# Second chunk's first unit of queries and keys by seven block products, its token sums made earlier

## The chip, the cores and the metric

The kernel runs as one program on one core of a Trainium2 chip. The metric is the device time of one execution in microseconds (us), the median of several runs. The engines are named as the profile names them: PE (matrix multiplication; PEld is its weight load), DVE (vector), ACT (scalar, activation functions), POOL and SP. SP only starts DMA transfers here. "SPq" is its queue of transfers.

## The reference, cut to what matters

The input is two sequences of 1024 tokens with 512 features, in float32. One block is computed:

```
xn = layernorm(x)
q, k, v = xn @ Wq.T + bq, xn @ Wk.T + bk, xn @ Wv.T + bv       # 32 heads of 16
s = softmax(causal(q k^T / 4)) v, heads joined, @ Wo.T + bo
g = silu(xn @ W_base.T + b_base + lora)                        # top 2 of 8 rank-16 experts
out = x + s * g
```

All large products are float32 products of a 512 x 512 weight with the tokens.

## The kernel before

**Chunks, units and steps.** Each sequence `b` is cut into two chunks `c` of 512 tokens, and the heads into four groups `oc` of eight. A unit `(b, oc, c)` is the attention of one head group over one chunk of queries. Its work is cut into steps: a unit with c = 0 has 5 steps, a unit with c = 1 has 13. The order of the first units is (0,0,0), (0,1,0), (0,0,1), (0,1,1): they take steps 0 to 4, 5 to 9, 10 to 22 and 23 to 35. In every step `n` the main loop issues, in this order, the score products (`scores(n)`, line 1392) with their two exponentials on ACT (line 1401), the products with the values of the step before (`values(n - 1)`, line 1442), the causal masks of step n on DVE (`masked(n)`, two multiplications `pt<-pt,causal`, only in steps on the diagonal), and then `fill(n)`. Every engine works through its own instructions in the order in which they were issued.

**Fill.** `fill(n)` (line 1298) puts tasks into the step: tasks with a cost in PE time, chosen by due step, and then tasks without one, which are DVE work and transfers. Projections (queries, keys, values, gate and output) are such tasks. They use a pool of two PSUM tiles (`mm_tile`, tag "mm"), so that a product can begin only when the tile of the product before the last has been read.

**Two ways to project queries and keys.** `qk_task` (line 377) makes the queries `pq` with four groups of four matmuls of 512 columns, the keys `pk` likewise, and ACT writes `qT` (two activations) and `kT` (one) from PSUM. `qk_blocks_task` (line 665) gets the same 2 x 2 block result with seven block products of 256 columns in place of eight, from sums of weight blocks (`four_sums`, four DVE operations on the tile `wqk`, by `qk_weights_task`, which also stores them with a transfer `kept<-wqk`) and sums of token blocks (`sums_task`, four DVE operations `asum2`, `asum1`, `asum0`, `asum3` of 128 x 512). DVE puts the products together:

```
p1 = product("q1", at(0, 0))
ve.tensor_scalar(keys[0], p1, bias, None, ALU.add)
add(q[0], product("q2", at(0, 1)), keys[0], less)
s = yield from sums_of(k)
add(keys[0], product("q6", s[1]), keys[0])
add(q[1], product("q7", s[2]), keys[0])
p5 = product("q5", s[0])
add(keys[0], p5, keys[0])
add(keys[1], p5, q[1])
add(keys[0], product("q3", s[3]), keys[0])
add(q[1], product("q4", at(1, 1)), q[1], less)
later.append((now[0] + 1, apart))
```

`apart` (line 705) is two activations on ACT, one after the other in place, that part `qT` into the two halves that the scores read. It is issued one step later, after that step's exponentials.

**Who uses which.** Before the change the first three units are projected whole: (0,0,0) by `first_task`, (0,1,0) and (0,0,1), which are `units[1:3]`, by `qk_task`. All others go through `stage` and `qk_blocks_task`. Block stages stand in `groups` (line 454); stages of one group share one set of token sums, made by the group's first stage. The first group is the values of chunk (0,1), a block product too (`p1` to `p7`), and the unit (0,1,1).

**The tokens of chunk (0,1).** `layernorm_task` normalizes them, turns them on DVE, writes them to a scratch tensor and reads them back in two halves as `xnT` (line 294, four transfers `xnT<-scr` for each half). `asum2` needs the first half alone, `asum1` the second half too.

Of the kernel before, what the change touches and what calls it, by code (L numbers as in the profile page):

```python
# [25 lines left out]
KC = D // P  # L26
# [54 lines left out]
def direct(ctx, tc, sound, x, wq, wk, wv, wo, wb, wa, wg, wB, bq, bk, bv, bo, bb, out):  # L81
# [34 lines left out]
    def load_qk(oc):  # L116


        t = sb.tile([P, 4 * KC, P], F32, tag="wqk", bufs=2, name=f"wqk{oc}")
        for n, src in enumerate((wq, wk)):  # L120
            nc.sync.dma_start(
                out=t[:, n * KC : n * KC + KC],
                in_=src.rearrange("(kc p) o -> p kc o", p=P)[:, :, oc * P : oc * P + P],
            )
        return t
# [79 lines left out]
    MM = 0.853  # L205
# [5 lines left out]
    turned_at, now = {}, [0]  # L211
# [165 lines left out]
    def qk_task(b, oc, c):  # L377

        xnT = xnTs[b, c]
        qk_begun.append((b, oc, c))  # L380
        pq = mm_tile("pq")
        for k in range(KC):
            matmul(
                pq, lhsT=wqks[oc][:, k, :], rhs=xnT[:, k, :], start=k == 0, stop=k == KC - 1
            )
            if k < KC - 1:
                yield MM
        qT = sb.tile([P, 2, C], F32, tag="qT", bufs=3, name=f"qT_{b}_{oc}_{c}")
        for par in range(2):
            nc.scalar.activation(  # L390
                qT[:, par], pq, AF.Identity, bias=bq_half[:, par, oc : oc + 1],
                scale=half[:, par : par + 1],
            )
        qTs[b, oc, c] = qT
        yield MM
        pk = mm_tile("pk")
        for k in range(KC):
            matmul(
                pk, lhsT=wqks[oc][:, KC + k, :], rhs=xnT[:, k, :], start=k == 0, stop=k == KC - 1
            )  # L400
            if k < KC - 1:
                yield MM
        kT = sb.tile([P, C], F32, tag="kT", bufs=4, name=f"kT_{b}_{oc}_{c}")
        nc.scalar.activation(kT, pk, AF.Identity, bias=bk_sb[:, oc : oc + 1])
        kTs[b, oc, c] = kT
        qk_done[b, oc, c] = now[0]
        yield MM
# [25 lines left out]
    def v_task(b, i):  # L433
# [18 lines left out]
    weights = {"v": (wv, bv_sb), "gate": (wb, bb_sb), "out": (wo, bo_sb)}  # L452

    groups = (
        [("v", 0, 1), ("qk", 0, 1, 1)],
        [("gate", 0, 0), ("qk", 0, 0, 2), ("qk", 0, 0, 3)],
        [("qk", 0, 1, 2), ("gate", 0, 1), ("qk", 0, 1, 3)],
        [("v", 1, 0), ("qk", 1, 0, 0), ("qk", 1, 0, 1)],
# [12 lines left out]
    combined, kept_at, b_diff, sums, sums_at, issued_at, ended = {}, {}, {}, {}, {}, {}, [0]  # L471
# [3 lines left out]
    def four_sums(at, to):  # L475

        ve.tensor_tensor(to[1], at[0, 1], at[0, 0], ALU.subtract)
        yield PAUSE
        ve.tensor_tensor(to[3], at[1, 1], at[0, 1], ALU.subtract)
        yield PAUSE  # L480
        ve.tensor_tensor(to[2], at[1, 1], to[1], ALU.subtract)
        yield PAUSE
        ve.tensor_tensor(to[4], at[1, 0], to[2], ALU.subtract)
# [41 lines left out]
    def qk_weights_task(n):  # L525

        oc = n % KC
        if n >= 2:
            wqks.append(load_qk(oc))
        w = wqks[n]  # L530
        sums = w[:, 2 * KC :]
        if n >= KC:
            nc.sync.dma_start(out=sums, in_=qk_kept[oc])
        else:
            for _ in range(3 if n >= 2 else 0):
                yield WAIT
            yield from four_sums(
                {(i, j): w[:, 4 * j + 2 * i : 4 * j + 2 * i + 2] for i in range(2) for j in range(2)},
                {t: sums[:, 2 * t - 2 : 2 * t] for t in range(1, 5)},
            )  # L540
            qk_kept[oc] = dram.tile([P, 2 * KC, P], F32, tag=f"kept_qk{oc}", bufs=1, name="kept")
            nc.sync.dma_start(out=qk_kept[oc], in_=sums)
        qk_ready[n] = now[0] + (2 if n >= KC else 0)
        yield WAIT
# [6 lines left out]
    def sums_task(k):  # L551

        at = tokens(k)
        s = [None] * 4

        def ahead(n):
            while k and made[k - 1] < n:
                yield WAIT

        def place(n):  # L560
            s[n] = sb.tile([P, 2, BK], F32, tag=f"sum{n}", bufs=1, name=f"asum{n}")
            return s[n]

        yield from ahead(4)
        ve.tensor_tensor(place(2), at(0, 0), at(1, 0), ALU.subtract)
        yield PAUSE
        ve.tensor_tensor(place(1), at(1, 1), s[2], ALU.subtract)
        yield PAUSE
        yield from ahead(5)
        ve.tensor_tensor(place(0), s[1], at(0, 0), ALU.add)  # L570
        yield PAUSE
        yield from ahead(6)
        ve.tensor_tensor(place(3), at(0, 1), s[1], ALU.subtract)
        group = group_of[stages[k]]
        sums[group], sums_at[group] = s, now[0]
# [291 lines left out]
    qk_begun = [(0, 0, 0)]  # L867
# [217 lines left out]
    units = [(b, oc, c) for b in range(NB) for oc in range(KC) for c in range(NC)]  # L1085
# [5 lines left out]
    plan, starts = [], {}  # L1091
# [50 lines left out]
    def normalized(b, c):  # L1142
        return sum(n < now[0] for n in posts.get((b, c), []))

    def stage(task, what, due, cost, takes, uses, ready, frees=()):

        k = stages.index(what)
        if what == groups[group_of[what]][0]:
            summed[k] = Task(
                due, sums_task(k), 0.0,  # L1150
                ready=lambda: ended[0] >= k - 1 and ready(),
            )

        def prepared():
            if what[0] == "qk":
                return now[0] > qk_ready.get(what[1] * KC + what[3], now[0])
            return issued_at.get((k, 1), now[0]) < now[0]

        staged[k] = Task(
            due, task(k), cost, takes=takes, uses=uses, frees=frees,  # L1160
            ready=lambda: ended[0] == k and ready() and prepared(),
        )
# [3 lines left out]
    for b in range(NB):  # L1166
        for c in range(NC):
            s0 = starts[b, 0, c]
            xn = [("xnT", b, c)]
# [3 lines left out]
            else:  # L1173
                Task(
                    s0 - 12 if b else -9, layernorm_task(b, c), 0.0, after=s0 - (40 if c == 0 else 30) if b else -9,
                    takes={"x": 1, "xnT": 1}, frees={"x": 1},
                )
            turned_ = lambda u=(b, c): now[0] > turned_at.get(u, now[0]) + 3
            for oc in range(KC):
                takes = {"qT": 1, "kT": 1}  # L1180
                if (b, oc, c) in units[1:3]:
                    Task(
                        starts[b, oc, c] - 1, qk_task(b, oc, c), 8 * MM, takes=takes, uses=xn,
                        ready=lambda u=units[units.index((b, oc, c)) - 1], t=turned_: u in qk_begun
                        and t(),
                    )
                elif oc or b or c:
                    stage(
                        qk_blocks_task, ("qk", b, c, oc), starts[b, oc, c] - 2, 7 * MM, takes, xn,
                        turned_,  # L1190
                    )
            if not b and not c:
                room["v"] -= 1
                for t in range(TT):
                    Task(
                        s0 + (1, 3, 5, 3)[t], v_task(b, t), 4 * MM, uses=xn + [("xnT", "wv")],
                        ready=turned_,
                    )
                Task(
                    3, combine_task("v", wv_sb), 0.0, after=5, uses=[("xnT", "wv")],  # L1200
                )
                for n, name in enumerate(("gate", "out")):
                    Task(
                        (20, 31)[n], combine_task(name), 0.0, after=(9, 22)[n], takes={"xnT": 1},
                        frees={"xnT": 1}, ready=lambda n=n: len(combined) > n,
                    )
                for n in range(2 * KC):
                    Task(
                        (20, 13, 26, 32)[n] if n < KC else -9, qk_weights_task(n), 0.0, after=9,
                        ready=lambda n=n: n < 2 or (  # L1210
                            now[0] > qk_done.get(((n - 2) // KC, (n - 2) % KC, 1), now[0])
                            and len(qk_ready) >= n
                        ),
                    )
            else:
                stage(values_task, ("v", b, c), s0 + (5 if c else 1), 14 * MM, {"v": 1}, xn, turned_)
# [4 lines left out]
                ready=turned_,  # L1221
# [3 lines left out]
                ready=lambda u=(b, c): now[0] > projected_at.get(u, now[0]),  # L1225
# [11 lines left out]
            else:  # L1237
                before = starts[b, KC - 1, c] + 2
                Task(len(plan) - 9, bases_task(b, c), 0.0, after=before - 12, takes={"xnT": 2})
                n = len(units) - 3  # L1240
# [3 lines left out]
                    ready=lambda: sum(len(x) for x in posts.values()) == len(units) - 1,  # L1244
                )
                for t in range(TT - 1):
# [9 lines left out]
                    ready=lambda b=b, c=c: normalized(b, c) == KC - 1,  # L1256
# [3 lines left out]
                    ready=lambda: posted.count(TT - 1) == 2,  # L1260
# [702 lines left out]
```

## Time and profile before

| what | us |
|---|---|
| median of 3 runs (601.55, 601.68, 602.28) | 601.68 |
| the profiled execution | 601.97 |
| its span, first to last instruction | 600.2 |
| PE busy in the span | 588.7 |
| DVE busy | 391.6 |
| ACT busy | 319.2 |

The time of an execution is 1.8 us more than the span of its instructions. Rows of a timeline give start, duration, engine, line, operation and tiles; "x8" rows are several instructions taken together, and square brackets hold the idle time of the engine before and what ended it. A float32 matmul has two records. The unit (0,0,1) is projected in the fill of step 8, from 59.07 to 66.05 us; the scores of step 8 start at 56.94, those of step 9 at 66.05, and those of step 10, the first that read the new queries, at 69.86.

### The profile page before, as it was taken

What the parts mean: (1) busy time and instruction counts of PE and PEld (TensorE: products, weight loads), DVE (VectorE), ACT (ScalarE), POOL (GpSimd) and SP (SyncE); (2) the same over time, 40 slices, a digit from 0 to 9 for tenths busy, and PEclk for the clock granted to TensorE, in tenths of its full rate; (3) what the DMA queues carried; (4) which work ended last, traced back from release to release, by engine and by line L of the source; (5) the groups of instructions that cost most, each with busy time, mean ns of one, the idle gap of its engine ahead of it and who ended that gap; (6) DMA issues with size and microseconds to landing.
All of it is one profiled execution on the core that took longest, in us unless ns stands there. A gap on an engine that the chain in (4) does not pass through costs nothing.

```text
span 600.2 us, 18801 instructions
## 1 busy us (share of the span) xinstructions
PE 588.7 (98%) x8327; PEld 281.9 (47%) x8327; DVE 391.6 (65%) x821; ACT 319.2 (53%) x368; POOL 9.2 (2%) x26
## 2 busy tenths in 40 slices
PE   8999999999999999999999999999999999999994
PEld 7335344544445544444346544453444454455551
DVE  4546788287488857566487866664547865785742
ACT  2445454656666565556655545455565565565631
POOL 2000000000001000000000000000000000000000
PEclk9999999999999999999999999999999999999998
DMA  8523474247101534234133062430121013401101
GB/s 266 140 69 122 136 261 149 55 142 211 39 4 48 189 109 129 89 101 135 36 111 90 22 194 80 159 125 6 37 71 52 11 51 98 161 21 55 58 20 58
DMA packets 57929, 58.66 MB, mean 98 GB/s; under 512 B 8312, under 2 KB 49280, under 8 KB 57456
## 3 DMA queue, kind: packets, MB, share of 16 engines
q1 hardware_dynamic: 57824, 57.38, 31.0%
q8 instruction: 67, 1.10, 0.8%
q14 instruction: 22, 0.18, 0.1%
q10 hardware_dynamic: 16, 0.00, 0.0%
HBM read 43.24 MB, written 14.12 MB: 96 GB/s over the span
## 4 chain that ended last, share of the span: by engine, by line
PE 93%; DMA 3%; DVE 3%; issue 0%; SPq 0%; ACT 0%; DVEq 0%
PE s L1392 25%; PE av L1442 23%; PE p L220 20%; PE q L220 13%; PE ph L220 3%; PE po L220 2%; PE pv L220 2%; DMA kept<-wqk 1%; PE pq L220 1%; PE pk L220 1%; DMA dens<-den 1%; DMA x<-in_x_dram 1%; DVE wqk L55 1%; PE pq_first L330 1%; PE h L220 1%; PE pk_first L330 0%
## 5 line engine op out<-in xcount | busy, mean ns | idle before, releaser
L1401 ACT ACTIVATE pt<-s 128x1024 f32<-128x1024 f32 x288 | 279.2, 1021 | 230.2 <-PE s L1392 228.6
L1392 PE MATMUL s<-qT,kT 32*128 32x512 f32 (+3 forms) x1680 | 166.5, 490 | 0.1
L1442 PE MATMUL av<-pt,v 128*32 128x512 f32 (+3 forms) x1680 | 154.3, 467 | 0.9 <-DVE pt L55 0.6
L55 DVE TENSOR_TENSOR pt<-pt,causal 128x512 f32<-128x512 f32 (+1 forms) x160 | 90.6, 582 | 64.9 <-ACT pt L1401 64.7
L1392 PEld LDWEIGHTS s<-qT,kT 32*128 32x128 f32 x1680 | 72.4, 184 | 68.3 <-issue 47.3
L1442 PEld LDWEIGHTS av<-pt,v 128*32 128x32 f32 x1680 | 39.7, 108 | 93.6 <-issue 61.4
L220 PE MATMUL p<-wt,asum 128*32 128x256 f32 x960 | 58.2, 379 | 0.0
L220 PE MATMUL q<-asum,wqk 128*32 128x256 f32 x832 | 50.8, 379 | 0.0
L220 PEld LDWEIGHTS p<-wt,asum 128*32 128x32 f32 x960 | 31.0, 110 | 26.5 <-issue 9.9
L220 PE MATMUL q<-xnT,wqk 128*32 128x256 f32 x624 | 40.2, 379 | 0.0
L220 PEld LDWEIGHTS q<-asum,wqk 128*32 128x32 f32 x832 | 27.0, 110 | 25.1 <-issue 8.4
L55 DVE TENSOR_TENSOR g<-p,g 128x512 f32<-128x512 f32 x28 | 18.9, 686 | 16.8 <-PE p L220 16.5
L220 PEld LDWEIGHTS q<-xnT,wqk 128*32 128x32 f32 x624 | 20.9, 110 | 18.9 <-issue 5.1
L220 PE MATMUL p<-w,xnT 128*32 128x256 f32 x448 | 27.3, 379 | 0.0
L55 DVE SCALAR_TENSOR_TENSOR kT<-q,kT 128x256 f32<-128x256 f32 x39 | 16.5, 422 | 14.9 <-PE q L220 14.3
L55 DVE TENSOR_TENSOR x<-p,x 128x512 f32<-128x512 f32 x21 | 14.2, 688 | 15.0 <-PE p L220 15.0
L55 DVE TENSOR_TENSOR v<-p,v 128x512 f32<-128x512 f32 x21 | 14.1, 687 | 11.2 <-PE p L220 11.2
L220 PE MATMUL p<-w,asum 128*32 128x256 f32 x320 | 20.0, 379 | 0.0
L220 PEld LDWEIGHTS p<-w,xnT 128*32 128x32 f32 x448 | 14.5, 110 | 11.1 <-issue 3.3
L747 ACT ACTIVATE sg<-g 128x512 f32<-128x512 f32 x16 | 10.0, 630 | 16.9 <-DVE g L55 16.9
L707 ACT ACTIVATE qT<-qT,half 128x512 f32<-128x512 f32 x26 | 18.8, 722 | 0.4
L220 PE MATMUL ph<-wag_sb,xnT 128*32 128x136 f32 x512 | 17.2, 279 | 0.0
(132 smaller groups left out, 479.4 us busy)
## 6 DMA issues: line engine op xcount, KB each, us to landing
wt<-kept SPq DMA_DIRECT2D x40, 256.0 KB
x<-in_x_dram SPq DMA_DIRECT2D x16, 256.0 KB
scr<-sq SPq DMA_DIRECT2D x6, 512.0 KB
xnT<-scr SPq DMA_DIRECT2D x24, 128.0 KB
w<-in_wb_dram SPq DMA_DIRECT2D x12, 256.0 KB
xr<-in_x_dram SPq DMA_DIRECT2D x12, 256.0 KB
out_dram<-x SPq DMA_DIRECT2D x12, 256.0 KB
w<-in_wv_dram SPq DMA_DIRECT2D x9, 256.0 KB
```

The source lines that it names most:

```text
L55: return getattr(self.engine, name)(*args, **named)
L220: nc.tensor.matmul(o[j : j + 32], lhsT=lhsT[:, j : j + 32] if len(lhsT.shape) == 2 else lhsT[:, j // 32], rhs=rhs, start=start, stop=stop,)
L330: nc.tensor.matmul(ps[:, cols], lhsT=w[:, k, :], rhs=xnT[:, k, cols], start=k == 0, stop=k == KC - 1)
L707: nc.scalar.activation(qT[:, par], qT[:, 0], AF.Copy, scale=half[:, par : par + 1])
L747: nc.scalar.activation(sg, g(i, j), AF.Tanh, scale=0.5)
L1392: nc.tensor.matmul(ss[s // 2][:, s % 2, col : col + w], lhsT=kT[rows, kt % TT * P : kt % TT * P + P], rhs=qTs[b, oc, c][rows, par, q0 : q0 ...
L1401: nc.scalar.activation(pt[:, 2 * pair : 2 * pair + 2], ss[pair], AF.Exp, scale=0.25)
L1442: nc.tensor.matmul(avs_now[par][32 * s : 32 * s + 32, q0 : q0 + w], lhsT=vs[b, kt][:, h * VS - HD * par : h * VS - HD * par + HP], rhs=pt[ ...
```

## The change

The unit (0,0,1) goes from `qk_task` to `qk_blocks_task`, as first stage of the first group. The values of chunk (0,1) come second and use the same token sums. The block stage of this unit is due one step before the unit's first step, others two steps. The token sums of the first group may start when two steps have gone by since the chunk was turned, not three. The weight sums of `wqk0` are due at step 7 and may start at step 5, not 20 and 9. All block stages of queries and keys now also wait until the unit before has begun its own.

```diff
     groups = (
-        [("v", 0, 1), ("qk", 0, 1, 1)],
+        [("qk", 0, 1, 0), ("v", 0, 1), ("qk", 0, 1, 1)],
...
             summed[k] = Task(
                 due, sums_task(k), 0.0,
-                ready=lambda: ended[0] >= k - 1 and ready(),
+                ready=lambda: ended[0] >= k - 1 and (ready() if k else now[0] > turned_at.get((0, 1), now[0]) + 2),
             )
...
-                if (b, oc, c) in units[1:3]:
+                if (b, oc, c) == units[1]:
                     Task(
                         starts[b, oc, c] - 1, qk_task(b, oc, c), 8 * MM, takes=takes, uses=xn,
...
                 elif oc or b or c:
                     stage(
-                        qk_blocks_task, ("qk", b, c, oc), starts[b, oc, c] - 2, 7 * MM, takes, xn,
-                        turned_,
+                        qk_blocks_task, ("qk", b, c, oc),
+                        starts[b, oc, c] - (1 if (b, oc, c) == units[2] else 2), 7 * MM, takes, xn,
+                        lambda u=units[units.index((b, oc, c)) - 1], t=turned_: u in qk_begun and t(),
                     )
...
-                        (20, 13, 26, 32)[n] if n < KC else -9, qk_weights_task(n), 0.0, after=9,
+                        (7, 13, 26, 32)[n] if n < KC else -9, qk_weights_task(n), 0.0, after=9 if n else 5,
```

In the order of the instructions, PE differs at one place: 56 matmuls of 256 columns (`q1`, `q2`, `q6`, `q7`, `q5`, `q3`, `q4`) stand where 32 of 512 columns (`pq`, `pk`) stood, in the fill of step 8. On DVE the weight sums `wqk0` come after the masks of step 6, the token sums after the masks of step 7 and so ahead of the masks of step 8, and the eight additions of the block products after the masks of step 8. On ACT three activations are gone, and `apart` stands after the exponentials of step 9, ahead of those of step 10. On SP `kept<-wqk0` and the loads of `wqk2` come earlier, and on DVE the routing work `hw`, `hsq` of chunk (0,0) does too.

## The prediction

> **What bounds the kernel now.** I read the page first: its busy times and the chain that ended last, and then what PE waited for.
>
> ```profile
> PE 588.7 (98%) x8327; PEld 281.9 (47%) x8327; DVE 391.6 (65%) x821; ACT 319.2 (53%) x368; POOL 9.2 (2%) x26
> ...
> PE 93%; DMA 3%; DVE 3%; issue 0%; SPq 0%; ACT 0%; DVEq 0%
> ```
>
> PE is busy for 98% of the span and carries 93% of the chain, so a microsecond of PE work taken away, or of waiting put in front of PE, moves the end by about as much. The waits of PE by cause show how little there is to win beside that:
>
> ```profile
> PE warm L170 <- POOL ident masks.py:199: 1.4, 1, 1.4
> ...
> PE av L1442 <- DVE pt L55: 0.6, 1, 0.6
> ```
>
> After the start-up PE waits once for long, 0.6 us at 92.30, for a mask. Then the timeline around the change, for PE, for DVE and for ACT:
>
> ```profile
> 59.07 3.62 PE L220 MATMUL pq<-xnT,wqk 128*32 128x512 f32 x32
> 62.51 3.62 PE L220 MATMUL pk<-xnT,wqk 128*32 128x512 f32 x32
> 66.05 1.15 PE L1392 MATMUL s<-qT,kT 32*128 32x256 f32 x16
> ...
> 69.86 1.14 PE L1392 MATMUL s<-qT,kT 32*128 32x512 f32 x8
> ```
>
> ```profile
> 59.18 0.69 DVE L55 TENSOR_TENSOR pt<-pt,causal 128x512 f32<-128x512 f32 x1 [1.39 <-ACT pt L1401]
> 60.10 0.69 DVE L55 TENSOR_TENSOR pt<-pt,causal 128x512 f32<-128x512 f32 x1 [0.22 <-ACT pt L1401]
> ...
> 64.17 0.69 DVE L55 TENSOR_TENSOR asum<-xnT 128x512 f32<-128x512 f32 x1
> 64.89 0.69 DVE L55 TENSOR_TENSOR asum<-xnT,asum 128x512 f32<-128x512 f32 x1
> 65.61 0.69 DVE L55 TENSOR_TENSOR asum<-asum,xnT 128x512 f32<-128x512 f32 x1
> 66.22 0.68 DVE L55 TENSOR_TENSOR asum<-xnT,asum 128x512 f32<-128x512 f32 x1
> ```
>
> ```profile
> 67.23 1.94 ACT L1401 ACTIVATE pt<-s 128x1024 f32<-128x1024 f32 x2 [0.35 <-DVE pr L55]
> ...
> 110.94 1.48 ACT L707 ACTIVATE qT<-qT,half 128x512 f32<-128x512 f32 x2
> ```
>
> The reader is to see three things. The whole products are two plain blocks on PE, from 59.07 to the scores of step 9 at 66.05, and nothing on DVE takes part. The masks of step 8 run at 59.18 and 60.10, and the token sums only after them. ACT is free after the exponentials of step 9, from 69.17.
>
> **Removed: one eighth of the PE work.** Two block products take 1.73 us on the chain (rows of `q` with 32 records), so one takes 0.865 and seven take 6.06. The whole products took 66.05 - 59.07 = 6.98. That is a gain of **0.92 us**.
>
> **Added: PE waits for DVE after the second product.** There are two PSUM tiles for these products. `q6` can begin only when DVE has read `q1`, and on DVE that reading stands behind the token sums and then the masks of step 8. So I follow DVE. The masks of step 6 end at 54.81. The four weight sums of `wqk0` follow; six such took 2.21 us in one row, so four take about 1.5 and end at 56.3, in the 1.37 us that DVE idles ahead of the masks of step 7 at 56.18. They cost nothing there: the 0.1 us of delay is covered by the values of step 7, which start at 58.19. The masks of step 7 end at 57.79, and `asum2` can run at once, as the first half of `xnT` has been there since 45.9.
>
> `asum1` needs the second half. The trace's records of finished transfers give 57.27, 58.06, 59.82 and 60.12 for its four transfers. The last of 16 parts came 1.02 us after the fifteenth (59.10). In the run before nobody felt it: PE reached that half at 60.79. Now DVE waits for it in order, and both masks behind it wait too. From 60.14, with the starts in the rows (0.72 us from one sum to one that depends on it, 0.61 otherwise, 0.60 to the next operation and between masks): `asum0` 60.86, `asum3` 61.47, masks 62.07 and 62.67, the addition of `q1` 63.28. The addition after two masks is in the trace too:
>
> ```profile
> 94.01 1.29 DVE L55 TENSOR_TENSOR pt<-pt,causal 128x512 f32<-128x512 f32 x2
> 95.22 0.48 DVE L55 TENSOR_SCALAR kT<-q,b_sb 128x256 f32<-128x256 f32 x1
> 95.80 0.48 DVE L55 SCALAR_TENSOR_TENSOR qT<-q,b_less,kT 128x256 f32<-128x256 f32 x1
> ```
>
> It lasts 0.48, so the tile is free at 63.76; PE starts 0.14 after DVE ends (mask end 92.16, values 92.30). `q6` starts at 63.90. It could have started at 59.07 + 1.73 = 60.80: **3.10 us** of waiting. The masks themselves hold nobody: their values come after the scores of step 9.
>
> After that products follow one another, except `q4`. It needs the tile of `q5`, which DVE reads twice. `q5` ends at 63.90 + 3 x 0.865 = 66.50; DVE begins 0.24 after the end of a product (97.22 + 0.865 to 98.33), the second reading ends 0.74 later (starts 102.24 and 102.57, 0.41 long), at 67.48, and `q4` starts at 67.62 in place of 67.36: **0.26 us**. The scores of step 9 start at 68.49, so 2.44 us late.
>
> **Added: the scores of step 10 wait for ACT.** Before, ACT wrote the queries at 62.76, long ahead. Now `apart` comes behind the exponentials of step 9 and is needed by the very next scores. Counted from the scores of step 9, the second exponential starts 2.10 later (68.15 - 66.05); an `apart` starts 0.905 after such a start (162.42 to 163.32) and lasts 1.48 in all; with 0.14 more PE starts at 4.63, where it started at 3.81: **0.81 us**. The two parts depend on one another and the scores read the one written last, so none of it is hidden.
>
> **Moved: the transfer that made the 0.6 us wait.** The chain shows where that wait comes from:
>
> ```profile
> 75.43 6.99 DMA kept<-wqk
> ...
> 84.03 5.01 DMA dens<-den
> ...
> 92.30 1.24 PE av L1442 x7
> ```
>
> SP stood at the load of `wqk2` until the sums of `wqk0` had been stored, and `dens<-den` was issued only after it. `rc` on DVE waited for that (0.51 us at 89.06), and `hw` and `hsq`, 1.4 us, stood ahead of the masks. With the change the sums are stored at about 59, the load follows at once, and `hw`, `hsq` come some 10 us sooner, where DVE idled 0.96 us at 77.59. The step from 90.56 to 95.26 took 4.70 where its work takes 3.79 (the step from 86.76), so **0.91 us** comes back. Bounds: nothing, if the queue holds `dens` up elsewhere, and 0.91; I take 0.91, as DVE would reach those masks by 90.5 and PE asks for them at 91.6.
>
> Edits at nothing: the earlier `kept<-wqk0` on SP (0.34 us of issue) stands ahead of the loads of `wt`, which wait for `kept<-wv` until 62.63 anyway and feed a product at 75.61; if that cover were gone it would cost its 0.34. The loads of `wqk2` (0.9 us of issue) stand ahead of `wt4`, needed at 88.72 and issued at 73.08. ACT loses one activation of 0.69. POOL has nothing new. The extra readiness condition leaves the order on PE as it was.
>
> **Sum.** -0.92 + 3.10 + 0.26 + 0.81 - 0.91 = **+2.34 us**. The profiled execution took 601.97 (span 600.2 and 1.77 around it), so 604.31; it stood 0.29 above the median of 601.68, against which the measured median is set, so **604.0**.
>
> **A rule that speaks against the change.** PE would idle 2.9 us in one piece (`q2`, held by the transfer to about 60.14, ends at 61.0). The trace's only drop of the clock comes after the last matmul ends at 592.66:
>
> ```profile
> 592.70:595.40 2.70, 0.00 (x0) 0.00 (x0) 1.60 (x4) 0.00 (x0) 0.00 (x0) 1.00 0.42 159
> 595.50:600.00 4.50, 0.00 (x0) 0.00 (x0) 0.00 (x0) 0.00 (x0) 0.00 (x0) 0.50 0.12 32
> ```
>
> The column PEclk (1.00, then 0.50) shows the drop at 595.47, after 2.81 us of idling, so by this row 2.9 us could be enough. The way back took 3.54 us at the start (matmuls from 1.42, full clock at 4.96): at half clock that loses at most 1.77 us. The Trainium skill, "TensorE: Matmul & The Clock Gate", section "What's actually happening", has the clock halved only after a whole idle window of 3413 ns that runs on its own; by it this gap costs nothing and the sum stays as it is. I leave the drop out of the sum and keep it as a rival.
>
> **Rivals.** *The tokens land in time* (not slower by what can be told). If the second half of `xnT` were there by 57.8, the chain on DVE would run through, the reading of `q1` would end at 62.13, and `q6` would wait 1.47 in place of 3.10: +0.71, 602.4. The late sixteenth part decides: the sum falls under 0.2% if the last transfer lands at 59.0 or sooner, and it did at 60.12. Fifteen parts by 59.10 speak for this case; that the transfers and what shares their rings up to then are the same in both kernels speaks against it.
>
> *DVE keeps up* (faster). Without either wait at the products and with 0.91 back, the sum is -1.02 (600.7) with the wait for `apart`, and -1.83 (599.9) without. It needs the additions of `q1` ahead of the masks or `apart` a step earlier, and the order of instructions has neither.
>
> *The clock drops.* 1.0 to 1.77 us on top, less what falls into the wait for `apart`: 605.0 to 605.8.
>
> **Numbers.** The forecast (603.0 to 604.9: the transfer up to 1.0 sooner, or the 0.91 not given back) has 0.70, the tokens in time 0.15, DVE keeping up 0.05, the clock 0.10. About 0.2% of this kernel (1.2 us) can be told from no change. Slower by more: 0.70 + 0.10 = 0.80; within: 0.15; faster by more: 0.05. The range takes in the forecast and reaches into the neighbours on both sides: 602.5 to 605.5.
>
> **What would show it.** Right: in the profile after, `asum1` starts near 60.1 with DVE waiting for `xnT<-scr`; PE idles some 2.9 us ahead of `q6`, named as a wait for DVE; the scores of step 9 start near 68.5, those of step 10 near 73.1 with PE waiting for ACT line 707; the 0.6 us wait for a mask near 95 is gone. Wrong: seven products in a row without a gap, scores of step 10 that follow `p1` at once, or a clock below 1.00 between 60 and 75.

## The result, and the profile after

The changed kernel is slower. Its four executions took 604.79, 605.39, 606.26 and 606.47 us, a median of 605.83, against 601.62 for the kernel before beside it (median of 4): a ratio of 1.0068 [1.0056, 1.0079] (its 95% interval in brackets), or +4.2 us where +2.3 was forecast. The median lies 0.33 above the top of the range. The profiled execution is the fastest of the four, 604.79 with a span of 603.0 (before: 601.97 and 600.2), so it is 2.8 longer than that of before, and the other three are longer still. The two parts of this have different causes, and they are read one after the other.

The page of the kernel after, its busy times and the chain that ended last:

```profile
PE 588.5 (98%) x8375; PEld 282.6 (47%) x8375; DVE 395.0 (65%) x829; ACT 318.3 (53%) x367; POOL 9.2 (2%) x26
...
PE 93%; DMA 2%; DVE 2%; ACT 1%; SPq 0%; issue 0%; DVEq 0%
```

PE has no more work than before (588.7), DVE has 3.4 more (it makes the sums and additions), and PE carries 93% of the chain as it did. So the 2.8 us are not work of PE; they must be waits. The waits of PE by cause in the kernel after:

```profile
PE q L220 <- DVE kT L55: 2.6, 1, 2.6
PE warm L170 <- POOL ident masks.py:199: 1.4, 1, 1.4
PE pt_x L319 <- DVE x L55: 0.9, 1, 0.9
PE s L1393 <- ACT qT L707: 0.7, 1, 0.7
PE q L220 <- DMA xnT<-scr: 0.5, 1, 0.5
```

Three of the rows shown are new, the first, the fourth and the fifth, and the 0.6 us wait of the values for a mask is gone. The timeline of PE around the change:

```profile
59.02 1.05 PE L220 MATMUL q<-xnT,wqk 128*32 128x256 f32 x16
60.56 1.07 PE L220 MATMUL q<-xnT,wqk 128*32 128x256 f32 x16 [0.49 <-DMA xnT<-scr]
64.20 3.66 PE L220 MATMUL q<-asum,wqk 128*32 128x256 f32 x64 [2.58 <-DVE kT L55]
67.97 1.07 PE L220 MATMUL q<-xnT,wqk 128*32 128x256 f32 x16
68.97 1.15 PE L1393 MATMUL s<-qT,kT 32*128 32x256 f32 x16
...
73.51 1.14 PE L1393 MATMUL s<-qT,kT 32*128 32x512 f32 x8 [0.66 <-ACT qT L707]
```

The rows are `q1`, `q2`, the four products from `q6` to `q3`, `q4`, and the scores of steps 9 and 10. `q6` starts at 64.20, where it would have followed `q2` at 61.4. What DVE did meanwhile:

```profile
57.66 0.68 DVE L55 TENSOR_TENSOR asum<-xnT 128x512 f32<-128x512 f32 x1
60.53 0.69 DVE L55 TENSOR_TENSOR asum<-xnT,asum 128x512 f32<-128x512 f32 x1 [2.19 <-DMA xnT<-scr]
61.26 0.69 DVE L55 TENSOR_TENSOR asum<-asum,xnT 128x512 f32<-128x512 f32 x1
61.86 0.68 DVE L55 TENSOR_TENSOR asum<-xnT,asum 128x512 f32<-128x512 f32 x1
62.47 1.29 DVE L55 TENSOR_TENSOR pt<-pt,causal 128x512 f32<-128x512 f32 x2
63.67 0.48 DVE L55 TENSOR_SCALAR kT<-q,b_sb 128x256 f32<-128x256 f32 x1
```

DVE stood 2.19 us at `asum1`, which waits for the second half of the tokens, and the last row, the reading of `q1` that PE needs, had `asum0`, `asum3` and both masks ahead of it. On ACT the parting of the queries comes between the exponentials of step 9 and the scores of step 10:

```profile
70.15 1.94 ACT L1402 ACTIVATE pt<-s 128x1024 f32<-128x1024 f32 x2 [10.14 <-PE s L1393]
71.98 1.48 ACT L707 ACTIVATE qT<-qT,half 128x512 f32<-128x512 f32 x2
```

It ends at 73.46 and the scores start at 73.51. In this execution the clock stayed at full speed (the column PEclk, 1.00) through both stretches that share the gap:

```profile
59.54:62.96 3.42, 1.60 (x28) 0.54 (x20) 2.40 (x4) 0.47 (x1) 0.00 (x0) 1.00 0.72 290
62.98:66.37 3.39, 2.17 (x40) 1.32 (x44) 2.24 (x6) 0.00 (x0) 0.00 (x0) 1.00 0.67 194
```

The second number of each row is PE's busy time in the stretch: 1.60 of 3.42 us, then 2.17 of 3.39. The stretches follow a grid that the traces show: where the clock falls in the middle of an execution (below), it is halved for 3.413 us or twice that, and the fall comes a whole number of such lengths after the clock first became full (17.0 of them from 5.79 to 63.82 us in the third run of this kernel). In this execution the clock became full at 4.93, so that one stretch runs from 59.54 to 62.95 and the next to 66.37. The mean clock of the four executions hints at why the other three are longer: 0.997 in this one, and 0.996, 0.994 and 0.993 in those of 605.39, 606.26 and 606.47.

### The profile page after: what moved, and what is told of

Its sections match the earlier page's. It is cut to its first block, busy times and chain, and to the rows that moved or that the text cites. A ratio compares the mean times of both kernels' runs of the same rounds, so it can differ in the third digit from the quotient of the medians.

```text
span 603.0 us, 18911 instructions
## 1 busy us (share of the span) xinstructions
PE 588.5 (98%) x8375; PEld 282.6 (47%) x8375; DVE 395.0 (65%) x829; ACT 318.3 (53%) x367; POOL 9.2 (2%) x26
## 4 chain that ended last, share of the span: by engine, by line
PE 93%; DMA 2%; DVE 2%; ACT 1%; SPq 0%; issue 0%; DVEq 0%
PE s L1393 25%; PE av L1443 23%; PE p L220 21%; PE q L220 14%; PE po L220 2%; PE pv L220 2%; PE ph L220 2%; DMA scr<-sq 1%; DMA x<-in_x_dram 1%; DMA xnT<-scr 1%; PE pq_first L330 1%; PE h L220 1%; PE pq L220 1%; PE pk L220 1%; PE pk_first L330 0%
## 5 line engine op out<-in xcount | busy, mean ns | idle before, releaser
L220 PE MATMUL q<-asum,wqk 128*32 128x256 f32 x896 | 54.4, 379 | 2.6 <-DVE kT L55 2.6
L220 PE MATMUL q<-xnT,wqk 128*32 128x256 f32 x672 | 43.1, 379 | 0.6 <-DMA xnT<-scr 0.5
L220 PEld LDWEIGHTS q<-asum,wqk 128*32 128x32 f32 x896 | 28.9, 110 | 29.4 <-issue 8.4
L707 ACT ACTIVATE qT<-qT,half 128x512 f32<-128x512 f32 x28 | 20.2, 722 | 0.5
```

What stands on the lines that cost most here:

```text
L220: nc.tensor.matmul(o[j : j + 32], lhsT=lhsT[:, j : j + 32] if len(lhsT.shape) == 2 else lhsT[:, j // 32], rhs=rhs, start=start, stop=stop,)
L707: nc.scalar.activation(qT[:, par], qT[:, 0], AF.Copy, scale=half[:, par : par + 1])
```

## The experiments

The theory to be tested has three parts. (1) PE is held at `q6` because the reading of `q1` stands behind work on DVE that itself waits for a transfer. (2) It is held again at the scores of step 10 by `apart`. (3) In some executions the gap of (1) also halves the clock. The rivals: the transfer doesn't matter, DVE's order alone does; block products of 256 columns are slower in themselves; the clock takes no part and the longer executions come from elsewhere.

**The masks first.** The order on DVE is changed and nothing else: `asum1` is issued after the masks of step 8, `asum0` after the addition of `q2`, `asum3` after that of `q6`.

```diff
# sums_task
+        if not k:
+            rest_of_sums.append(lambda: ve.tensor_tensor(place(1), at(1, 1), s[2], ALU.subtract))
+            rest_of_sums.append(lambda: ve.tensor_tensor(place(0), s[1], at(0, 0), ALU.add))
+            rest_of_sums.append(lambda: ve.tensor_tensor(place(3), at(0, 1), s[1], ALU.subtract))
+            sums[group_of[stages[k]]], sums_at[group_of[stages[k]]] = s, now[0]
+            return
# qk_blocks_task, at three places: ahead of the addition of q1, behind that of q2, behind that of q6
+        next_sum(k)      # for k == 0: rest_of_sums.pop(0)()
```

> The changed kernel, but of the four token sums only asum2 stands ahead of the masks of step 8; asum1 follows the masks, asum0 the addition of q2, asum3 that of q6. Theory (masks behind a sum that waits for a transfer hold the second product's successor): q6 starts near 61.9 where it started at 64.2, 0.3 after q2 ends, scores of step 9 near 66.4, the wait for the parted queries (0.7) stays, 0.9 from the earlier weight sums stays: +0.3 to +0.6 on before, 602.0, and no fall of the clock. Rival (PE is held by the pool of two PSUM tiles whatever the order on DVE): 604 or above.

Measured: 602.31 (median of 11) against 601.74 of the kernel before beside it, 1.0009 [0.9998, 1.0019]; the changed kernel run again beside both took 604.84 (median of 6). Rows of DVE and of PE in its timeline:

```profile
60.86 0.68 DVE L55 TENSOR_TENSOR asum<-xnT,asum 128x512 f32<-128x512 f32 x1
61.46 0.48 DVE L55 TENSOR_SCALAR kT<-q,b_sb 128x256 f32<-128x256 f32 x1
```

```profile
60.56 1.07 PE L220 MATMUL q<-xnT,wqk 128*32 128x256 f32 x16 [0.28 <-DMA xnT<-scr]
62.00 3.66 PE L220 MATMUL q<-asum,wqk 128*32 128x256 f32 x64 [0.37 <-DVE kT L55]
...
66.77 1.15 PE L1408 MATMUL s<-qT,kT 32*128 32x256 f32 x16
...
71.30 1.14 PE L1408 MATMUL s<-qT,kT 32*128 32x512 f32 x8 [0.66 <-ACT qT L722]
```

The reading of `q1` starts at 61.46 in place of 63.67 and `q6` at 62.00 in place of 64.20. The two intervals after it, from `q6` to the scores of step 9 (4.77) and on to those of step 10 (4.53), are those of the changed kernel. So 2.2 us of the wait were the order on DVE, and the products in themselves cost nothing more than the sum said.

> The changed kernel once more, for the spread of its runs. Its profiled execution (604.79) is 2.8 us slower than the profile of before and is explained by the timeline, but its median (605.83) lies 1.0 above that. Theory A (clock): in some executions the half-idle stretch ahead of q6 makes the clock of PE fall for one window, 1.0 to 1.8 us; then the slow executions are those with the lower mean clock (0.993 or 0.994 where the profile has 0.997), in a group at 606.2 to 606.5. Theory B (transfer): the executions differ by the time at which the second half of xnT lands; then the times spread evenly and the mean clock does not follow them.

The changed kernel again, with its clocks: 604.55 (0.997), 603.33 (0.996), 605.47 (0.994), 604.81 (0.996), 607.26 (0.994), 604.87 (0.996); ratio 1.0060 [1.0043, 1.0078]. The spread of 3.9 us is several times that of the masks-first kernel (602.03 to 602.92 over 11 executions, no clock below 0.995), so it comes with the long wait at `q6`. The two executions at 0.994 took 605.47 and 607.26, not 606.2 to 606.5 as theory A had it, and those at 0.996 and 0.997 spread over 1.5 us by themselves, so the clock is not the only thing that differs.

**No wait for the transfer.** The order stays that of the changed kernel; `asum1` and `asum3` of the first group read the first half of the tokens twice.

```diff
-        ve.tensor_tensor(place(1), at(1, 1), s[2], ALU.subtract)
+        ve.tensor_tensor(place(1), at(1, 1 if k else 0), s[2], ALU.subtract)
...
-        ve.tensor_tensor(place(3), at(0, 1), s[1], ALU.subtract)
+        ve.tensor_tensor(place(3), at(0, 1 if k else 0), s[1], ALU.subtract)
```

> The changed kernel, in which the second and fourth token sum of the first group read the first half of the tokens in place of the second, so that no sum waits for a transfer (this part of the result is not the reference's). The order on DVE is that of the changed kernel: four sums, two masks, then the reading of q1. Theory (two causes on top of one another, the transfer and the order): asum1 starts at 58.4 in place of 60.5, the reading of q1 ends near 62.0, q6 starts near 62.1 where it started at 64.2; PE idles 0.6 us in place of 2.6, the clock stays up; 2.1 under the undisturbed 604.8: 602.7. Rival (the order on DVE alone makes the wait, sums and masks being 4.0 us of DVE work however early they start): q6 after 63.5, 604 or more.

Measured: 602.86 (median of 8) against 601.53, 1.0024 [1.0014, 1.0034]. Rows of its timeline, DVE and PE:

```profile
60.42 1.29 DVE L55 TENSOR_TENSOR pt<-pt,causal 128x512 f32<-128x512 f32 x2
61.63 0.48 DVE L55 TENSOR_SCALAR kT<-q,b_sb 128x256 f32<-128x256 f32 x1
```

```profile
62.16 3.66 PE L220 MATMUL q<-asum,wqk 128*32 128x256 f32 x64 [0.35 <-DVE kT L55]
```

With the same queue on DVE but nothing in it that waits, `q6` starts at 62.16. The order alone is therefore not enough for the 2.6 us wait: it takes a queue and a late transfer at its head. Counted as in the prediction, from `q1` and two products on, `q6` waits 3.45 us in the changed kernel, 1.04 with the masks first and 1.30 here: either remedy takes out most of it. (The second half of the tokens is left out of two of the sums, so the result is not the reference's; the number and the size of the operations are the same.) This is also the case that the prediction kept as "the tokens land in time": +1.3 measured against the 0.71 worked out for it.

**A longer hold.** The fourth token sum is made three times ahead of the masks: forecast as 1.2 us more of DVE, in the trace 1.45 (2.14 for the three, 0.68 for the one).

```diff
+        for _ in range(0 if k else 2):
+            ve.tensor_tensor(s[3], at(0, 1), s[1], ALU.subtract)
```

> The changed kernel with the fourth token sum made three times, two more DVE operations (1.2 us) ahead of the masks of step 8, so that PE idles 3.8 us in one piece ahead of q6 where it idles 2.6 us. Without any effect of the clock: 604.8 + 1.2 = 606.0. Theory A (clock falls when one window of about 3.4 us is idle for the most part): now in nearly every execution, the profile shows PEclk at 0.5 for some 3.4 us from a point between 63 and 67, mean clock 0.994 or less, 607.0 to 607.8. Theory B (transfer alone sets the spread): 606.0, PEclk stays at 1.00 in the profile and the mean clock at 0.996 or 0.997.

Measured: 607.65 (median of 4) against 601.48, 1.0105 [1.0090, 1.0120]; the changed kernel beside it took 604.89 (median of 5). The wait grew to 4.0, and the clock fell in the profiled execution; its windows:

```profile
62.24:65.64 3.40, 0.12 (x4) 0.12 (x8) 3.22 (x7) 0.00 (x0) 0.00 (x0) 1.00 0.55 185
65.66:69.05 3.39, 3.39 (x36) 1.74 (x34) 0.82 (x2) 0.00 (x0) 0.00 (x0) 0.50 0.54 163
```

PE worked 0.12 us in one stretch of 3.40, and in the next, equally long, the granted clock was 0.50 although PE was busy throughout. All four executions had a mean clock of 0.992 to 0.994. Added to the 604.6 that the changed kernel takes without a drop (below), 1.45 for the DVE work and 1.69 for one drop make 607.7.

**The changed kernel a third time.**

> The changed kernel once more, beside the next one. So far ten executions: the four with a mean clock of 0.994 or less took 605.5 to 607.3, the six with 0.996 or more 603.3 to 605.4. Theory A: the same two groups, about 1.7 apart, some four in ten in the slow one; median 605.0 to 605.5. Theory B: no such groups, times and clock unrelated.

Measured: 605.26 (0.994), 604.89 (0.996), 605.17 (0.994), 604.72 (0.997), 603.72 (0.996); ratio 1.0052 [1.0038, 1.0066]. Its profiled execution, 605.26, is one of those with a low clock, and shows the drop inside the kernel as submitted. PE's timeline, then the windows:

```profile
63.08 5.35 PE L220 MATMUL q<-asum,wqk 128*32 128x256 f32 x64 [2.11 <-DVE kT L55]
68.54 1.07 PE L220 MATMUL q<-xnT,wqk 128*32 128x256 f32 x16
69.54 1.15 PE L1393 MATMUL s<-qT,kT 32*128 32x256 f32 x16
```

```profile
60.40:63.80 3.40, 1.29 (x28) 0.55 (x24) 3.11 (x6) 0.00 (x0) 0.00 (x0) 1.00 0.52 195
63.83:67.22 3.39, 3.39 (x40) 1.68 (x36) 0.85 (x2) 0.00 (x0) 0.00 (x0) 0.50 0.78 249
```

Here the tokens landed sooner (59.19 against 60.31), so `q6` could start 1.1 earlier and the wait is shorter, 2.11 instead of 2.58. Yet the four products behind it took 5.35 in place of 3.66, and the scores of step 9 came 0.57 later than in the execution without a drop. From `q6` to the scores it is 6.46 instead of 4.77: one drop costs 1.69 us. It follows a stretch in which PE still worked 1.29 us, while the stretch of the first profile that worked 1.60 kept the clock. The landing matters too: this execution has a drop and an early landing, and its time, 605.26, does not stand out.

Of the 15 executions of the changed kernel in all, six have a mean clock of 0.994 or less and take 605.17 to 607.26; nine have 0.996 or more and take 603.33 to 605.39. The means are 606.0 and 604.6, 1.4 apart; the two groups overlap, and the median of this run, 604.89, lies just under the 605.0 to 605.5 of theory A. The nine spread over 2.1 us, which the drop can't explain; landings of the tokens as far apart as the two seen (1.1 us) would do half of it, but only profiled executions show when they land. By the mean clock the first four hold two of the six, a little more than their share, and their median, 605.83, is higher than that of all 15, 604.89. In 57 executions of the kernel before there is one of 0.994 and none lower; in the 30 of the three kernels that wait less than 0.9 us at `q6` in their profile (masks first, no wait for the transfer, and "both" below) none is under 0.995.

**Keep PE busy.** If the drop needs an idle PE, matmuls that nobody reads, put between `q2` and `q6`, should prevent it and leave the wait for DVE.

```diff
+        if not k:
+            idle = ps_s.tile([P, 2, C], F32, tag="s", name="idle")
+            for m in range(2):
+                matmul(idle[:, m % 2], lhsT=w[:, 0], rhs=xnTs[0, 0][:, 0, :], start=True, stop=True)
```

> The changed kernel with 8 matmuls of 512 columns more (1.7 us of PE, result unused) between q2 and q6, where PE idles 2.6 us in the profile after. Everything else waits as before. Theory A (clock): the idling is filled, the clock stays up, so the median falls to the profiled execution's 604.8 (604.5 to 605.2), the spread to under 0.8 us, and no execution has a mean clock under 0.996: work added makes the kernel faster. Theory B (transfer): median stays at 605.8 or above, and the spread stays.

> The changed kernel with 1.7 us of unused matmuls in the idle stretch ahead of q6, once more, beside the changed kernel itself. Theory A: no execution in a slow group, median 604.7 and 0.3 to 0.7 under the changed kernel. Theory B: the same median and spread as the changed kernel.

Measured: 604.76 (median of 5) against 601.74, 1.0057 [1.0044, 1.0070], and again 605.02 (median of 5) against 601.48, 1.0066 [1.0052, 1.0080]. PE's timeline in the first of them:

```profile
61.45 1.93 PE L220 MATMUL idle<-xnT,wqk 128*32 128x512 f32 x16
64.24 3.66 PE L220 MATMUL q<-asum,wqk 128*32 128x256 f32 x64 [0.86 <-DVE kT L55]
```

`q6` starts where it did, so PE's own work is not what delays it, and the profile has no drop. Only one of the ten executions has a clock of 0.994 or less (606.7 at 0.993), against six of 15. But the median did not come down 0.3 to 0.7 below that of the changed kernel (604.84 and 604.89 beside it), as it should have, and this expectation was missed. The lists of executions show where part of it went: all ten are 1.9 to 2.5 us longer than their span, all 15 of the changed kernel 1.7 to 1.8; why is not known. By spans the mean is 602.9 against 603.4, and the median 602.9 against 603.1. These runs speak for the clock's part mainly by how often it falls.

**Part the queries at once.** `apart` is issued in the fill of step 8, ahead of the exponentials of step 9; once in the changed kernel, and once together with the masks first ("both").

```diff
-        later.append((now[0] + 1, apart))
+        if k:
+            later.append((now[0] + 1, apart))
+        else:
+            apart()
```

> The changed kernel with the masks ahead of asum1 (as in the run with the masks first, 602.3) and with the parting of the queries issued at once after the last product, ahead of the exponentials of step 9, while ACT is idle. Theory (the scores of step 10 wait for the parting, which waits for the exponentials): that wait of 0.66 to 0.73 goes and the exponentials of step 9, some 1.2 us later, still end before the scores of step 10 need their PSUM tiles: 601.5, about as before. Rival (the later exponentials hold the scores of step 10 instead): 602.3.

> The changed kernel with the parting of the queries issued at once after the last product, ahead of the exponentials of step 9; the token sums stay ahead of the masks. Theory: the wait of 0.66 of the scores of step 10 goes, the wait of 2.6 ahead of q6 and the falls of the clock stay: 0.65 to 0.73 under the changed kernel (median 604.9 over fifteen executions), 604.2, with single executions 1.7 above that. Rival (the exponentials of step 9 come later and hold step 10): 604.9.

Measured, both: 601.68 (median of 11) against 601.48, 1.0002 [0.9993, 1.0011]. Its row of ACT, and of PE at the scores of step 10:

```profile
68.00 1.48 ACT L722 ACTIVATE qT<-qT,half 128x512 f32<-128x512 f32 x2 [7.19 <-DVE qT L55]
```

```profile
67.35 1.15 PE L1411 MATMUL s<-qT,kT 32*128 32x256 f32 x16
...
71.16 1.32 PE L1411 MATMUL s<-qT,kT 32*128 32x512 f32 x8
...
75.14 1.14 PE L1411 MATMUL s<-qT,kT 32*128 32x512 f32 x8
```

ACT parts the queries as soon as DVE has made them, and the scores of step 10 follow without a wait, 3.81 after those of step 9, as before the change. The rival came true in part: the scores of step 10 last 1.32 where they took 1.14, and step 11 starts 3.98 after them where it started 3.80 (73.66 - 69.86 before the change), so 0.18 of the 0.73 is paid there again. Both waits are mended here as far as the order goes, and the kernel is just level with the one before, though it also has the transfer's gift of 0.9.

The parting alone took 605.15 (median of 6) against 601.53, 1.0054 [1.0040, 1.0068], no different from the changed kernel. Its median says little about the parting, because the clock was low in at least three of its six executions (0.990, 0.992, 0.994); the two with 0.998 and 0.997 took 603.66 and 604.31. Its profile shows that the wait is gone there too: the scores of step 10 start 3.80 after those of step 9 (75.86 - 72.06). The profiled one, 606.95, lost two stretches; its windows:

```profile
60.43:63.82 3.39, 1.19 (x20) 0.50 (x16) 2.79 (x5) 0.06 (x1) 0.00 (x0) 1.00 0.72 290
63.84:67.24 3.40, 2.57 (x25) 1.20 (x29) 1.68 (x4) 0.00 (x0) 0.00 (x0) 0.50 0.70 222
67.26:70.65 3.39, 3.39 (x37) 1.56 (x33) 0.99 (x3) 0.00 (x0) 0.00 (x0) 0.50 0.25 86
```

**The weight sums alone.** The kernel before with only the earlier weight sums of `wqk0`, and no block products for this unit.

```diff
-                        (20, 13, 26, 32)[n] if n < KC else -9, qk_weights_task(n), 0.0, after=9,
+                        (7, 13, 26, 32)[n] if n < KC else -9, qk_weights_task(n), 0.0, after=9 if n else 5,
```

> The kernel before with one part of the change alone: the weight sums of wqk0 due at step 7 and allowed from step 5; queries and keys of (0,0,1) stay whole products. Theory (dens is queued behind the load of wqk2, which waits for the stored sums): the wait of 0.6 us for a mask near 92 goes, the step there takes 3.8 in place of 4.7, all else stays: 0.9 faster, 600.8. Rival (that wait only moves, to another transfer or to the sums of wqk2): within 0.3 of before, 601.6.

> The kernel before with the early weight sums alone, once more, to see whether it is faster than the kernel before beyond doubt. Theory: the profile shows no wait for a mask near 92, 0.7 to 0.9 under the kernel before, 600.8. Rival (the first comparison, 0.9991 with 0.9982 to 1.0000, was the luck of its runs): within 0.3 of before.

Measured: 600.98 (median of 11) against 601.74, 0.9991 [0.9982, 1.0000], and again 600.97 (median of 11) against 601.53, 0.9989 [0.9980, 0.9998]. Rows of DVE and PE in the second:

```profile
88.55 0.34 DVE L55 RECIPROCAL rc<-dens 128x32 f32<-128x32 f32 x1
...
90.57 0.75 DVE L55 TENSOR_TENSOR pt<-pt,causal 128x256 f32<-128x256 f32 x2
```

```profile
90.87 1.15 PE L1392 MATMUL s<-qT,kT 32*128 32x384 f32 x16
91.95 1.06 PE L1442 MATMUL av<-pt,v 128*32 128x512 f32 x8
...
94.67 1.14 PE L1392 MATMUL s<-qT,kT 32*128 32x512 f32 x8
```

`rc` no longer waits for `dens` (0.51 us before), the masks start 1.2 us sooner than in the kernel before, and the values follow their scores without the 0.6 us wait: the step takes 3.80 instead of 4.70. The first interval just reaches 1, the second stays under it. This one line is the best version of all that were run, the only one ahead of the kernel before.

## Why the prediction was wrong, and where it was right

The sum against the profiled execution. The measured column is read from starts of scores: step 9 moved from 6.98 to 9.95 after the first product, step 10 from 3.81 to 4.54 after step 9, and the shift at step 16 is 0.90 less than at step 10.

| term | predicted | measured | where |
|---|---|---|---|
| seven products for eight | -0.92 | -0.79 | 7 x 0.865 and 0.13 from the last product to the scores, against 6.98 |
| waits ahead of `q2` and `q6` | +3.10 | +3.45 | 0.675 (60.56 - 59.885) and 2.775 (64.20 - 61.425) |
| wait of `q4` | +0.26 | +0.31 | 67.97 - 64.20 - 4 x 0.865 |
| `apart` ahead of step 10 | +0.81 | +0.73 | 4.54 - 3.81 |
| the mask wait near 92 | -0.91 | -0.90 | 3.65 at step 10, 2.75 at step 16 |
| exponentials of steps 128 and 129 | none | +0.28 | 536.17 - 533.14, less 2.75 |

The measured terms add up to 3.08, the forecast was 2.34. Less the 0.05 by which `q1` starts sooner, that is the 3.03 of the shift from step 130 on; the last matmul of PE starts 3.01 later (595.45 against 592.44), and 0.2 comes back behind it, so the span is 2.8 longer. Of the 1.8 us between the forecast, 604.0, and the median, 605.83, 0.5 is this sum (604.31 forecast for the profiled execution, 604.79 measured), 0.3 is the allowance for a profiled execution above the median, which the new one was not, and 1.0 is the distance from that execution up to the median.

**Right in kind.** All five mechanisms are there, in the places and with the signs that were forecast. Runs bear out three of them one by one. The masks first and the run without the transfer wait came out 2.5 and 2.0 below the changed kernel, for 2.4 and 2.15 less of the wait at `q6`. The weight sums alone came out 0.6 to 0.8 below before, for 0.90 in the trace. "Both" came out 0.4 below the masks first, each against its own runs of before, for 0.73 less 0.18; this is the weakest of the three. The seven products and the wait of `q4` are read from the timeline alone. The mask wait went where the queue said: to nothing, without a new wait behind it.

**Wrong: "I leave the drop out of the sum and keep it as a rival", with a chance of 0.10.** It happens in about six of 15 executions, by their mean clock, and costs some 1.4 (the two means) to 1.69 (the one trace), so about 0.6 on average where the sum had nothing. Two drops among the first four put their median 1.0 above its own profiled execution, and so above the range. That it left the range was luck in part: the median of all 15, 604.89, lies within it. The row of before that I had weighed was nearer the mark than I allowed: a drop after 2.81 us of idling, with a gap of 2.9 forecast. And it held more than I read. From the first full clock (4.96) to the drop (595.47) it is 173.0 lengths of 3.413 us, and the last of these stretches was not wholly idle:

```profile
592.05:595.47 3.42, 0.61 (x10) 0.13 (x2) 1.99 (x5) 0.00 (x0) 0.00 (x0) 1.00 0.35 132
595.47:598.88 3.41, 0.00 (x0) 0.00 (x0) 0.00 (x0) 0.00 (x0) 0.00 (x0) 0.50 0.14 41
```

PE was busy for 0.61 us of it, and the clock fell at its end. I had set the row aside for the Trainium skill, "TensorE: Matmul & The Clock Gate", section "What's actually happening". It says that the gate counts in windows of 3413 ns which run on their own, and that the clock is halved after at least one idle window. The first half agrees with the traces: the stretches at half clock last 3.413 us or twice that, on the grid told above. The second half does not, if an idle window is one without any work, as I read it: a window with PE busy for 0.61 us lost the clock in the kernel before, and one with 1.29 in the changed kernel. I also should have used what free-running windows mean. The forecast had one clock for all executions, but whether a gap of this length falls into one window, as in the third run, or is shared by two, as in the first profile, differs from execution to execution, so it is a price paid at a rate, and it moves a median of few.

**Too small: 3.10 for the wait.** The last transfer landed at 60.31, not 60.12, and DVE started `asum1` 0.22 after that, not 0.02: 0.39 later in all. `q1` started 0.05 sooner than before, and PE took up `q6` 0.05 after the end of DVE's row, not 0.14: 0.39 + 0.05 - 0.09 make the 0.35. That `q2` was held by the transfer adds nothing, since it still ended long before `q6` could begin.

**Too large by 0.13: the seven products.** 6.98 held the hand-over from the last product to the scores; 6.06 did not. The two sides of a difference have to end at the same event.

**Not foreseen: 0.28 from step 130 on.** The exponentials of step 128 start 1.52 us after their scores in place of 1.23, in the changed kernel, with PE kept busy, with the masks first, with the longer hold and without the transfer wait, but not in both, the parting alone, or the weight sums alone. An `apart` and the exponentials of step 129 follow them on ACT and are late by the same, and so is PE at step 130. The traces tell where this comes from, though not why. In every trace of these five kernels the exponentials of steps 51, 91 and 128 are late in this way, and the first of each pair is number 192, 320 or 448 of the 509 records that ACT has in the trace with its waits, so they stand 128 records apart. The kernels without the delay have 508 or 511 records on ACT, and the first exponentials of these steps have other numbers. So the delay goes with the place in ACT's sequence of instructions, which the change moved by two records; what happens there stays open.

**Of the rivals**, *the tokens land in time* did not come true in the first profile, and came half true in the third (59.19); *DVE keeps up* needed an order that the change doesn't have, and even where that order was made, with the masks first, the kernel did not get ahead of the one before, for 1.0 us of waits at the products remains (`q6` starts at 62.00, `q1` at 59.23, and two products take 1.73).

## What to carry to other kernels

When products are handed to an engine that adds them up, the first reading behind a pool of two tiles is on the path, and every instruction queued ahead of it, with the latest transfer any of those wait for, is part of its price: issue the reading first and the sums that wait last. A PE gap of 2 us or more (2.11 was enough once) deserves its own look at the granted clock in several executions, since the cost of a drop shows up as a spread between them rather than in one profile. And a change of several parts should be run part by part: here one moved line was worth 0.6 to 0.8 us and the rest of the change used it up.

## What the runs showed of the hardware

The clock falls without a wholly idle window. Windows of 3.4 us with PE busy for 0.12, 0.61, 1.19 and 1.29 us were followed by one at half clock, and so was one with 1.33 (594.10 to 597.52 us, at the end of the second run with PE kept busy); with 1.60 the clock stayed. In the run with the parting alone a window at half clock in which PE was busy for 2.57 of 3.40 us was followed by a second at half clock, and one with PE busy throughout (3.39 at half clock in the third row there) by full clock. The boundary between 1.33 and 1.60 was not measured more closely, and other things than PE's busy time may count.

The last of the 16 parts of the transfer that `asum1` waits for landed 0.6 to 1.6 us after the fifteenth in all 13 profiled executions. It landed 60.12 to 60.78 us from the start of the span in twelve of them and at 59.19 in one, 0.87 after the fifteenth, an execution of the changed kernel. What makes it late was not tried.
